# Two row tiles' sources moved into the first span of a graph-attention layer, and its settling scaled on ScalarE

## The chip, the cores and the metric

The kernel runs on one core of a Trainium2 chip. The metric is the device time of one execution in microseconds (us). Engines are named as in the profile: PE is TensorE's matmuls and PEld its weight loads, DVE is VectorE, ACT is ScalarE, POOL is GpSimd, SP is SyncE (here it issues most DMAs). A line number such as L1225 is a line of the kernel before.

## The reference, cut to what matters

Two layers run on 2708 nodes with 256 features. Each layer adds its result to its input and normalizes each row. Layer 0 is a diffusion with top-p attention; it is untouched by the change and only its last rows matter here. Layer 1 is a graph attention with four heads of 64:

```python
Wh = jnp.einsum('nd,hdo->nho', x, W)
s_i = jnp.einsum('nho,ho->nh', Wh, a_src)
s_j = jnp.einsum('nho,ho->nh', Wh, a_dst)
e = jax.nn.leaky_relu(s_i[:, None, :] + s_j[None, :, :], NEG_SLOPE)
mask = (adj.at[idx, idx].set(1.0) != 0)[:, :, None]
attention = jax.nn.softmax(jnp.where(mask, e, -jnp.inf), axis=1)
h_prime = jnp.einsum('ijh,jho->iho', attention, Wh)
x = _layernorm(x + h_prime.reshape(n, h * fo), axis=-1)
```

So every output row i is a sum over all source nodes j, divided by its softmax denominator per head, added to x and normalized.

## The kernel before, in words

The 2708 rows are cut into 22 row tiles: 16 of 128 rows and 6 of 110. `xe` holds x of all tiles in SBUF; layer 0 overwrites it tile by tile with its own result.

**End of layer 0.** The work of layer 0 is written as generators that a hand-made schedule advances slot by slot. `finish` (L919) is the last one of each tile: residual sums on GpSimd, two layernorms that go between VectorE (statistics L935, L936, output L944) and GpSimd (L940, the root L941), and then `sources` (L137). `sources` prepares a tile as a source of layer 1: TensorE transposes x (L142), ScalarE copies the transpose (L144), TensorE multiplies by the weights (L148), ScalarE writes the exponentials `sb` and `tj`, the scores `s_src` and the scaled values (L152 to L158), and SP stores the values in DRAM (L161). Its two PSUM tiles come from layer 0's pool `tr`.

**Layer 1.** Output rows are taken in three spans of 8, 8 and 6 row tiles (1024, 1024 and 660 columns). For each span the kernel goes over all 22 source tiles; the first span takes them in the order `first` (tiles 8 to 19, then 0 to 7, then 20 and 21). For each source tile:

- SP loads a block of the adjacency (L1164, three buffers `blk`), ScalarE makes a mask of it with Sign and Square (L1165, L1170), and where the block has the diagonal GpSimd sets it between the two (L1168, L1169);
- VectorE makes four products `pt`, one for each head (L1225), in two sets of buffers;
- TensorE accumulates the values (L1233, eight matmuls that use 64 columns of the array) and the denominators (L1240, eight that use 32 columns), in six PSUM banks `acc`.

`targets` (L167) prepares a span's rows: for each row tile four transposes (L174) into an `aux` bank and two exponentials on ScalarE (L179). For span 0 it runs in layer 0's last tile; for the next span it is called at the middle of a span (L1217). There are two `aux` banks in all.

At the end of a span ScalarE and VectorE copy the accumulators to SBUF as `val` and `den` (L1248 to L1250). `settle` (L1173) then finishes the span's row tiles. It is called at the third source tile of the next span (L1211), so that it lies beside that span's work, and at the very end for the last span (L1252). For each row tile: three transposes into an `aux` bank (L1180, L1181), the reciprocal of the denominators (L1183) and the scaling (L1187) on VectorE, the residual on GpSimd (L1192), layernorm (statistics L126 and L128 on VectorE, L130 and the root L132 on GpSimd, output L133 on VectorE), and a store by SP (L1195).

**What sets the order.** Each engine works through its own list in order. In layer 1 that list is made by a scheduler when the kernel is built, which can set an instruction ahead of the place where it is written: `targets` of span 1 is written at the middle of span 0, and in the list before it stands ahead of the span's first matmul, between the sources of the last tiles. A matmul that waits holds up all that stand behind it on TensorE.

A second, general version of layer 0 is run afterwards if a flag asks for it (L1261); with these inputs it is not run.

Of the kernel before, what the change touches and what calls it, by code (L numbers as in the profile page):

```python
# [16 lines left out]
P = 128  # L17
# [28 lines left out]
def kernel(  # L46
# [87 lines left out]
            dst, src, mv[:m, 0:1], rs[:m], op0=ALU.subtract, op1=ALU.mult  # L134
        )

    def sources(t, pool, ps):  # L137

        m = rows[t]
        tp = ps.tile([P, 4, P], F32, name="tr")  # L140
        for c in range(DC):
            nc.tensor.transpose(tp[:, c, :m], xe[:m, t, c * P : (c + 1) * P], ident[:m, :m])  # L142
        xT = pool.tile([P, DC, P], F32, name="xT")
        nc.scalar.copy(xT[:, :, :m], tp[:, 0:DC, :m])  # L144
        yield
        wp = ps.tile([P, 4, P], F32, name="tr").rearrange("p a b -> p (a b)")
        for c in range(DC):
            nc.tensor.matmul(  # L148
                wp[:m, : D + 2 * H], xT[:, c, :m], wx[:, c, :],
                start=(c == 0), stop=(c == DC - 1),  # L150
            )
        nc.scalar.activation(sb[:m, t, :], wp[:m, D : D + H], AF.Exp)  # L152
        nc.scalar.activation(tj[:m, t, :], wp[:m, D : D + H], AF.Exp, scale=NEG_SLOPE - 1.0)
        nc.scalar.copy(s_src[:m, t, :], wp[:m, D + H : D + 2 * H])
        vt = pool.tile([P, D], F32, name="cs")
        for h in range(H):
            cols = slice(h * FO, (h + 1) * FO)
            nc.scalar.activation(  # L158
                vt[:m, cols], wp[:m, cols], AF.Copy, scale=sb[:m, t, h : h + 1]
            )  # L160
        nc.sync.dma_start(vd[t][:m], vt[:m])  # L161
# [322 lines left out]
    def fast_layer0(ep, adjp):  # L484
# [434 lines left out]
        def finish(t, ac, ca, cb):  # L919

            m = rows[t]
            xt = xe[:m, t, 0:D]
            xw = rowp.tile([P, D], F32, name="xw")[:m]
            nc.scalar.activation(xw, ac[:m, :D], AF.Copy, scale=rinv[:m, t : t + 1])  # L924
            yield
            while t not in held:
                yield
            hh = heldp.tile([P, D], F32, name="hh", bufs=4)[:m]
            nc.gpsimd.tensor_add(ca[:m], ca[:m], cb[:m])
            nc.gpsimd.tensor_add(ca[:m], ca[:m], held.pop(t)[:m])  # L930
            nc.gpsimd.tensor_add(hh, ca[:m], xw)
            yield
            for last in range(2):
                st, mv = small.tile([P, 6], F32, name="ln_st")[:m], small.tile([P, 2], F32, name="ln_mv")[:m]
                nc.vector.bn_stats(st, hh)  # L935
                nc.vector.bn_aggr(mv, st)  # L936
                yield
                yield
                ve, rs = new("ln_ve", m), new("ln_rs", m)
                nc.gpsimd.tensor_scalar(ve, mv[:, 1:2], LN_EPS, None, op0=ALU.add)  # L940
                nc.gpsimd.tensor_tensor(rs, ve, minus_half[:m], op=ALU.pow)  # L941
                yield
                yield
                nc.vector.tensor_scalar(  # L944
                    xt if last else hh, hh, mv[:, 0:1], rs, op0=ALU.subtract, op1=ALU.mult
                )
                yield
                yield
                if not last:
                    nc.gpsimd.tensor_mul(hh, hh, g_sb[:m])  # L950
                    nc.gpsimd.tensor_add(hh, hh, b_sb[:m])
                    nc.gpsimd.tensor_add(hh, hh, xt)
                    yield
                    yield
            yield from sources(t, rowp, ps_tr)


# [30 lines left out]
                ),  # L988
            )

        ahead = []

        def step(s, cur, spend):
            for t in range(NT):
# [132 lines left out]
            bad, pt[0:1, 0:1], -1.0, float(2 * NT * P), op0=ALU.mult, op1=ALU.add  # L1127
        )
        l0.close()
        return ahead  # L1130

# [1 line left out]

    def layer1(ep, adjp, r):
        l1 = ExitStack()

        pp, rp, pj, keep = (
# [31 lines left out]
        def settle(g, val, den):  # L1173

            for t in spans[g]:
                m = rows[t]
                cols = slice(off[t] - off[spans[g][0]], off[t + 1] - off[spans[g][0]])
                u = ps_u.tile([P, H, P], F32, name="aux")
                for q in range(2):
                    nc.tensor.transpose(u[:m, q, :], val[:, q, cols], ident)  # L1180
                nc.tensor.transpose(u[:m, 2, :], den[:, cols], ident)  # L1181
                rden = small.tile([P, H], F32, name="rden")
                nc.vector.reciprocal(  # L1183
                    rden[:m], u[:m, 2, :].rearrange("p (h o) -> p h o", h=H)[:, :, 0]
                )
                res = pp.tile([P, H, FO], F32, name="res")
                nc.vector.tensor_tensor(  # L1187
                    res[:m], u[:m, 0:2, :].rearrange("p q (h o) -> p (q h) o", h=2),
                    rden[:m].unsqueeze(2).to_broadcast([m, H, FO]), op=ALU.mult,
                )  # L1190
                flat = res[:m].rearrange("p h o -> p (h o)")
                nc.gpsimd.tensor_add(flat, flat, xe[:m, t, 0:D])  # L1192
                o = pp.tile([P, D], F32, name="o")
                layernorm(o[:m], flat, m)
                nc.sync.dma_start(out[off[t] : off[t + 1], :], o[:m])  # L1195
# [5 lines left out]
        for g, span in enumerate(spans):  # L1201
            gw = off[span[-1] + 1] - off[span[0]]
            cuts = [(c, min(CHUNK, gw - c)) for c in range(0, gw, CHUNK)]
            acc = [
                [ps_v.tile([P, CHUNK], F32, name=f"acc{k}_{c}") for c in range(len(cuts))]
                for k in range(3)
            ]
            for n, j in enumerate(range(NT) if g else first):
                k = rows[j]
                if n == 2 and due:  # L1210
                    settle(*due)  # L1211
                if n == NT // 2 and g + 1 < len(spans):
                    if g % 2:
                        r_next = room(ep)
                    else:
                        r_next = [rp.tile([P, 2, GW], F32, name=f"r{q}") for q in range(2)]
                    list(targets(g + 1, r_next, aux))  # L1217
                if g == 0:
                    nc.sync.dma_start(v[j][:k].rearrange("p h o -> p (h o)"), vd[j][:k])
                mask = neighbours(g, j)  # L1220
                at = dict(start=(n == 0), stop=(n == NT - 1), skip_group_check=True)
                pts = []
                for h in range(H):
                    pt = pj.tile([P, GW], F32, name=f"pt{h}")
                    nc.vector.scalar_tensor_tensor(  # L1225
                        pt[:k, :gw], r[h // 2][:k, h % 2, :gw], tj[:k, j, h : h + 1], mask,
                        op0=ALU.max, op1=ALU.mult,
                    )
                    pts.append(pt)
                    if h % 2 == 1:  # L1230
                        for c, (c0, w) in enumerate(cuts):
                            for q in range(2):
                                nc.tensor.matmul(  # L1233
                                    acc[h // 2][c][q * FO : (q + 1) * FO, :w],
                                    v[j][:k, h - 1 + q, :],
                                    pts[h - 1 + q][:k, c0 : c0 + w], **at,
                                )
                for c, (c0, w) in enumerate(cuts):
                    for h in range(H):
                        nc.tensor.matmul(  # L1240
                            acc[2][c][h * 32 : (h + 1) * 32, :w],
                            sb[:k, j, h : h + 1].to_broadcast([k, 32]), pts[h][:k, c0 : c0 + w], **at,
                        )
            r = r_next
            val = pp.tile([P, 2, GW], F32, name="val")
            den = pp.tile([P, GW], F32, name="den")
            for c, (c0, w) in enumerate(cuts):
                nc.scalar.copy(val[:, 0, c0 : c0 + w], acc[0][c][:, :w])  # L1248
                nc.vector.tensor_copy(val[:, 1, c0 : c0 + w], acc[1][c][:, :w])
                nc.scalar.copy(den[:, c0 : c0 + w], acc[2][c][:, :w])  # L1250
            due = (g, val, den)
        settle(*due)  # L1252
        l1.close()
# [1 line left out]
    with ExitStack() as both:  # L1255

        adjp = both.enter_context(tc.tile_pool(name="adjp", bufs=3))
        ep = both.enter_context(tc.tile_pool(name="ep", bufs=3))
        layer1(ep, adjp, fast_layer0(ep, adjp))
    flag = nc.values_load(bad[0:1, 0:1])  # L1260
    with tc.If(flag > 0):  # L1261
        general_layer0()
        with ExitStack() as again:
            adjp = again.enter_context(tc.tile_pool(name="adjp", bufs=3))
            ep = again.enter_context(tc.tile_pool(name="ep", bufs=3))
            layer1(ep, adjp, None)


# [43 lines left out]
```

## Time and profile before

| what | before |
|---|---|
| median of three runs | 1677.54 us (1677.26 to 1679.2) |
| the profiled execution | 1677.58 us, of which the profile's span is 1675.8 us |
| layer 1's first matmul | 1298.14 us from the span's start |
| last matmul of the last span | ends near 1653.8 us |
| last output row tile written by VectorE | ends at 1668.76 us |

Times inside the profile are counted from the span's start. In the chain of waits each line gives start, length, engine, the tile written and the line. In lists by engine, "x16" counts profile records; a matmul of float32 has two records, a transpose one. The share of time an engine is busy is an average over stages with different limits, so the stages of layer 1 (1298 to 1676 us) are looked at one by one.

### The profile page before, as it was taken

How to read it: one execution, taken by the hardware profiler on the slowest of the kernel's cores; microseconds unless marked ns; L12 is line 12 of the kernel's file. 1: busy time of each engine (PE TensorE's matmuls, PEld its weight loads, DVE VectorE, ACT ScalarE, POOL GpSimd, SP SyncE). 2: the span in 40 equal slices, each digit the busy share in tenths (PEclk: the TensorE clock that was granted, in tenths of full speed). 3: DMA queues.
4: the chain of work that ended last, by engine and by line, in shares of the span. 5: the costliest groups of instructions: out<-in, count | busy, mean ns of one | idle time of the engine just before them, and what ended most of it. 6: DMA issues, size and time to landing. Idle time of an engine off the chain costs nothing.

```text
span 1675.8 us, 23985 instructions
## 1 busy us (share of the span) xinstructions
PE 1610.0 (96%) x8218; PEld 1058.0 (63%) x8218; DVE 1217.0 (73%) x3660; ACT 766.8 (46%) x1324; POOL 423.4 (25%) x893
## 2 busy tenths in 40 slices
PE   7999999999999999999999999999997999999895
PEld 4677777777777776777787878777785222322332
DVE  2954554565455019888999999998994899888886
ACT  1333333333333255656576666667555334243231
POOL 0310111111011023223244444444434020420313
PEclk9999999999999999999999999999999999999998
DMA  6211011111110142212322322323222332232231
GB/s 166 73 47 46 26 43 40 40 31 40 40 43 25 43 104 67 63 49 73 79 72 79 87 68 82 89 58 77 72 65 88 98 99 86 88 93 77 76 86 39
DMA packets 153873, 113.89 MB, mean 68 GB/s; under 512 B 39898, under 2 KB 144094, under 8 KB 153742
## 3 DMA queue, kind: packets, MB, share of 16 engines
q1 hardware_dynamic: 149278, 105.18, 23.4%
q0 software_dynamic: 2112, 5.55, 1.0%
q10 hardware_dynamic: 2352, 1.54, 0.3%
q8 instruction: 67, 1.10, 0.3%
q14 instruction: 64, 0.52, 0.1%
HBM read 101.16 MB, written 11.09 MB: 67 GB/s over the span
## 4 chain that ended last, share of the span: by engine, by line
PE 78%; DVE 9%; ACT 5%; POOL 4%; issue 3%; DMA 0%; ACTq 0%; POOLq 0%; DVEq 0%; SPq 0%
PE att L217 23%; PE walk L845 19%; PE acc L1233 12%; PE acc L1240 6%; PE lg L620 5%; PE tr L202 4%; ACT e L624 3%; PE tr L910 2%; PE tr L890 2%; PE lg L1056 1%; PE tr L591 1%; DVE cand L725 1%; ACT eT L208 1%; DVE scr L791 1%; POOL res L1192 1%
## 5 line engine op out<-in xcount | busy, mean ns | idle before, releaser
L645 ACT ACTIVATE junk<-e,minus,rth 128x2708 bf16<-128x2708 f32 (+1 forms) x88 | 232.8, 2646 | 35.7 <-POOL rth L677 34.6
L845 PE MATMUL walk<-xe,blk 128*128 128x257 f32 (+3 forms) x968 | 240.5, 382 | 0.0
L217 PE MATMUL att<-ba,eT 128*128 128x256 f32 (+3 forms) x968 | 234.1, 383 | 5.0 <-ACT eT L208 5.0
L217 PE MATMUL att<-xe,eT 128*128 128x256 f32 (+3 forms) x968 | 233.3, 381 | 4.3 <-ACT eT L208 4.3
L208 ACT COPY eT<-tr 128x512 f32<-128x512 f32 (+5 forms) x264 | 138.2, 537 | 206.3 <-PE tr L202 206.1
L1233 PE MATMUL acc<-pt,v 128*64 128x512 f32 (+3 forms) x1056 | 226.0, 550 | 4.7 <-DVE pt L1225 3.8
L845 PE MATMUL walk<-yw,blk 128*128 128x256 f32 (+3 forms) x968 | 228.1, 381 | 1.7 <-ACT xw L924 1.7
L725 DVE MAX8 cand<-e 128x8 f32<-128x170 f32 (+1 forms) x352 | 89.2, 322 | 178.8 <-ACT e L624 178.8
L845 PEld LDWEIGHTS walk<-xe,blk 128*128 128x128 f32 (+3 forms) x968 | 174.6, 186 | 54.2 <-issue 29.3
L845 PEld LDWEIGHTS walk<-yw,blk 128*128 128x128 f32 (+3 forms) x968 | 176.7, 186 | 41.5 <-issue 11.5
L1225 DVE SCALAR_TENSOR_TENSOR pt<-e,tj,blk 128x1024 f32<-128x1024 f32 (+3 forms) x176 | 185.8, 1115 | 19.8 <-issue 8.0
L217 PEld LDWEIGHTS att<-ba,eT 128*128 128x128 f32 (+3 forms) x968 | 171.4, 186 | 32.7 <-ACT eT L208 10.0
L217 PEld LDWEIGHTS att<-xe,eT 128*128 128x128 f32 (+3 forms) x968 | 170.9, 186 | 30.9 <-ACT eT L208 7.2
L624 ACT ACTIVATE e<-lg 128x1024 f32<-128x1024 f32 (+1 forms) x132 | 121.1, 921 | 132.3 <-PE lg L620 132.3
L1233 PEld LDWEIGHTS acc<-pt,v 128*64 128x64 f32 (+1 forms) x1056 | 72.1, 137 | 153.5 <-issue 112.3
L202 PE MATMUL tr<-ident,e 128*128 128x128 f32 (+3 forms) x968 | 140.8, 270 | 4.6 <-ACT xT L606 3.8
L202 PEld LDWEIGHTS tr<-ident,e 128*128 128x128 f32 (+3 forms) x968 | 115.1, 139 | 32.3 <-ACT xT L606 6.1
L1165 ACT ACTIVATE blk<-blk 128x1024 f32<-128x1024 f32 (+3 forms) x66 | 63.2, 958 | 155.3 <-DMA blk<-in_adjT_dram 136.3
L1240 PE MATMUL acc<-pt,sb 128*32 128x512 f32 (+3 forms) x1056 | 124.5, 549 | 0.0
L1225 DVE SCALAR_TENSOR_TENSOR pt<-r,tj,blk 128x1024 f32<-128x1024 f32 (+1 forms) x88 | 109.8, 1306 | 10.8 <-issue 7.0
L631 POOL TENSOR_TENSOR fact<-zp 128x1 f32<-128x1 f32 (+1 forms) x44 | 24.8, 563 | 359.0 <-ACT e L624 349.1
L725 DVE MAX8 cand<-scr 128x8 f32<-128x97 f32 (+1 forms) x616 | 101.9, 243 | 0.0
(203 smaller groups left out, 1999.6 us busy)
## 6 DMA issues: line engine op xcount, KB each, us to landing
blk<-in_adjT_dram SPq DMA_DIRECT2D x32, 704.0 KB
blk<-in_adjT_dram SPq DMA_DIRECT2D x32, 512.0 KB
blk<-in_adjT_dram SPq DMA_DIRECT2D x48, 330.0 KB
blk<-in_adjT_dram SPq DMA_DIRECT2D x32, 320.0 KB
blk<-in_adjT_dram SPq DMA_DIRECT2D x12, 605.0 KB
blk<-in_adjT_dram SPq DMA_DIRECT2D x12, 440.0 KB
blk<-in_adjT_dram SPq DMA_DIRECT2D x18, 283.6 KB
c<-cs POOLq DMA_DIRECT2D x32, 128.0 KB, 2.1
```

The costliest lines, as they stand in the source:

```text
L202: nc.tensor.transpose(tr[: rows[t], q, :m], e[:m, off[t] : off[t + 1]], ident[:m, :m])
L208: copy(eT[:k, : len(grp), :m], tr[:k, : len(grp), :m])
L217: nc.tensor.matmul(acc, eT[: rows[t], q, :m], value(t), start=(t == 0), stop=(t == NT - 1),)
L620: nc.tensor.matmul(lg[:m, h, :w], qT[part, cols], kT[s][part, c0 : c0 + w], start=True, stop=True,)
L624: nc.scalar.activation(halves[:m, :, c0 : c0 + w], lg[:m, :, :w], AF.Exp, accum_out=zp[:m, n : n + 1],)
L645: nc.scalar.activation(junk[:m], e[:m], func, scale=rth, bias=minus1[:m], accum_out=acc)
L725: nc.vector.max(cand[:, n, :], src[:m, n * size : min(N, (n + 1) * size)])
L845: nc.tensor.matmul(ac[:m, :w], blk[: rows[j], j - j0, :m], cur[: rows[j], j, 0:w], start=(j == 0), stop=(j == NT - 1),)
L1165: nc.scalar.activation(bar, bar, AF.Sign)
L1225: nc.vector.scalar_tensor_tensor(pt[:k, :gw], r[h // 2][:k, h % 2, :gw], tj[:k, j, h : h + 1], mask, op0=ALU.max, op1=ALU.mult,)
L1233: nc.tensor.matmul(acc[h // 2][c][q * FO : (q + 1) * FO, :w], v[j][:k, h - 1 + q, :], pts[h - 1 + q][:k, c0 : c0 + w], **at,)
L1240: nc.tensor.matmul(acc[2][c][h * 32 : (h + 1) * 32, :w], sb[:k, j, h : h + 1].to_broadcast([k, 32]), pts[h][:k, c0 : c0 + w], **at,)
```

## The change

The change has these parts.

- For the fast layer 0, `sources` of the last two row tiles (20 and 21) is not called at the end of `finish`. It is called in layer 1, at the third source tile of span 0, with layer 1's pools: the PSUM tiles are `aux` banks.
- `settle` scales on ScalarE: four activations of 64 columns for each row tile, with the reciprocal as scale, in the place of one VectorE instruction.
- In the last span's `settle` each of the six row tiles has a PSUM bank of its own (the `acc` banks, which are free by then), and the residual is added on VectorE. In the other spans GpSimd keeps it.
- Of the two copies of the denominators at the end of a span, the second moves from ScalarE to VectorE.

```diff
@@ finish
+            if t in late:
+                return
             yield from sources(t, rowp, ps_tr)
@@ fast_layer0
-        ahead = []
+        ahead, late = [], (NT - 2, NT - 1)
@@ settle
-                u = ps_u.tile([P, H, P], F32, name="aux")
+                if g < len(spans) - 1:
+                    u = aux()
+                else:
+                    n = t - spans[g][0]
+                    u = ps_v.tile([P, CHUNK], F32, name=f"acc{n // 2 % 3}_{n % 2}")
+                    u = u.rearrange("p (h m) -> p h m", h=H)
...
-                res = pp.tile([P, H, FO], F32, name="res")
-                nc.vector.tensor_tensor(
-                    res[:m], u[:m, 0:2, :].rearrange("p q (h o) -> p (q h) o", h=2),
-                    rden[:m].unsqueeze(2).to_broadcast([m, H, FO]), op=ALU.mult,
-                )
-                flat = res[:m].rearrange("p h o -> p (h o)")
-                nc.gpsimd.tensor_add(flat, flat, xe[:m, t, 0:D])
+                flat = pp.tile([P, D], F32, name="res")[:m]
+                for h in range(H):
+                    nc.scalar.activation(
+                        flat[:, h * FO : (h + 1) * FO],
+                        u[:m, h // 2, (h % 2) * FO : (h % 2 + 1) * FO],
+                        AF.Copy, scale=rden[:m, h : h + 1],
+                    )
+                adder = nc.vector if g == len(spans) - 1 else nc.gpsimd
+                adder.tensor_add(flat, flat, xe[:m, t, 0:D])
@@ layer1, over the source tiles
                 if n == 2 and due:
                     settle(*due)
+                if n == 2 and g == 0:
+                    for t in late:
+                        for _ in sources(t, pp, ps_u, "aux"):
+                            pass
@@ layer1, end of a span
-                nc.scalar.copy(den[:, c0 : c0 + w], acc[2][c][:, :w])
+                copy = nc.vector.tensor_copy if c else nc.scalar.copy
+                copy(den[:, c0 : c0 + w], acc[2][c][:, :w])
```

More of the change, by code (lines that the diff above doesn't have):

```diff
@@ L135, in layernorm, with sources @@
         )
-    def sources(t, pool, ps):
+    def sources(t, pool, ps, name="tr"):
         m = rows[t]
-        tp = ps.tile([P, 4, P], F32, name="tr")
+        tp = ps.tile([P, 4, P], F32, name=name)
         for c in range(DC):
@@ L145, in sources @@
         yield
-        wp = ps.tile([P, 4, P], F32, name="tr").rearrange("p a b -> p (a b)")
+        wp = ps.tile([P, 4, P], F32, name=name).rearrange("p a b -> p (a b)")
         for c in range(DC):
@@ L1129, in fast_layer0, with layer1 @@
         l0.close()
-        return ahead
-    def layer1(ep, adjp, r):
+        return ahead, late
+    def layer1(ep, adjp, r, late):
         l1 = ExitStack()
@@ L1258 @@
         ep = both.enter_context(tc.tile_pool(name="ep", bufs=3))
-        layer1(ep, adjp, fast_layer0(ep, adjp))
+        layer1(ep, adjp, *fast_layer0(ep, adjp))
     flag = nc.values_load(bad[0:1, 0:1])
@@ L1265 @@
             ep = again.enter_context(tc.tile_pool(name="ep", bufs=3))
-            layer1(ep, adjp, None)
+            layer1(ep, adjp, None, ())
 _ARGS = [
```

## The prediction

> **What bounds the kernel now.** I read the profile in this order: busy shares, busy time by stage, the chain of work that ended last in the three places the edits touch, and the order of instructions on each engine there.
>
> ```profile
> PE 1610.0 (96%) x8218; PEld 1058.0 (63%) x8218; DVE 1217.0 (73%) x3660; ACT 766.8 (46%) x1324; POOL 423.4 (25%) x893
> ```
>
> TensorE is the average bound, but the edits lie where it is not. By stage (columns: length, then busy PE, PEld, DVE, ACT, POOL, clock, DMA share, GB/s):
>
> ```profile
> 1298.10:1428.60 130.50, 130.46 (x768) 35.60 (x768) 116.30 (x96) 52.89 (x54) 15.00 (x16) 1.00 0.33 95
> 1428.60:1472.90 44.30, 42.92 (x204) 13.33 (x200) 35.62 (x60) 12.14 (x19) 20.17 (x28) 1.00 0.28 85
> 1472.90:1562.60 89.70, 89.70 (x556) 25.77 (x552) 80.55 (x70) 36.20 (x43) 9.42 (x12) 1.00 0.30 85
> 1562.60:1603.10 40.50, 35.73 (x222) 13.55 (x218) 31.34 (x64) 9.79 (x13) 15.14 (x24) 0.96 0.27 77
> ```
>
> Rows 1 and 3 are plain stretches of layer 1: a row tile takes TensorE 5.44 us, back to back. Rows 2 and 4 are where the previous span is settled. There five row tiles take 44.3 us (5.44 each would be 27.2) and, up to 1599.47, 36.9 us (3.62 each: 18.1), although TensorE has only 24 settling transposes to add, some 3 us. So each settling costs about 14 us. The chain says why (start, us, what):
>
> ```profile
> 1564.30 1.93 POOL res L1192 x2
> 1566.23 0.02 issue
> 1566.26 0.43 DVE ln_st L126
> ...
> 1568.63 0.41 DVE o L133
> 1569.05 0.34 DVE res L1187
> 1569.39 0.07 issue
> 1569.46 1.94 POOL res L1192 x2
> ...
> 1591.33 0.97 PE acc L1240 x2
> ```
>
> Scale on VectorE, residual on GpSimd, statistics, root on GpSimd, output, next scale: a serial round of 5.16 us for two row tiles (5.54 in row 2), in which VectorE passes one `pt` product (L1225). The last line is a second loss: a denominator matmul alone among numerators. At the handover from layer 0 and at the end:
>
> ```profile
> 1294.42 0.42 DVE xe L944
> 1294.84 0.04 issue
> 1294.88 0.41 PE tr L142 x2
> ...
> 1298.14 1.90 PE acc L1233 x7
> ```
>
> ```profile
> 1660.71 0.71 POOL res L1192
> ...
> 1662.29 0.41 DVE o L133
> ```
>
> Layer 1's first matmul waits for the last tile's x, and in the tail two tiles go round every 4.55 us (`o` at 1657.74, 1662.29, 1666.85).
>
> **What the Trainium skill says.** *TensorEngine Tiling (Array Packing)*, Key Properties: column tiles run in parallel, and changing the tiling mode drains TensorE. The trace agrees: eight 64-column matmuls take 3.59 us (0.90 a pair), four 32-column ones 0.93, a lone one 0.97. *SBUF — State Buffer*, Who interferes with whom: a VectorE instruction with two SBUF inputs and a GpSimd one that reads SBUF block each other. Agrees: `ln_ve` takes 0.22 us, but 1.16 beside a `pt` (at 1450.32). No page prices the new ScalarE scaling better than L158, the same form: four in 0.80 us.
>
> **First span.** Two kinds of work move. Sources of tiles 20 and 21: on TensorE 2 transposes (0.25 us with their gap) and 2 matmuls (0.9 to 1.1) each; on ScalarE 8 instructions (1.4 us); on SP a store and a load, now behind mask loads five and six, with over a dozen row tiles until those two are used. And what moved without being named: the 32 transposes and 16 exponentials of `targets` for span 1. Today they run while TensorE waits for x of tiles 20 and 21 (3.89 us idle before 1288.40 alone); in the new order they stand at the span's twelfth tile.
> - *Start.* In the new order only tile 20's transposes stand before the first matmul: x is there at 1288.3, the second `pt` at 1289.4, so matmuls start near 1289.45, 8.7 us earlier. But VectorE's order is unchanged: `pt` three and four end at 1292.3 and 1293.6 (a bn_stats waiting for GpSimd is in front), the next four at 1296.0 to 1299.6. The new order also sets a lone denominator matmul inside the first two tiles (0.97 each). First tile done 1297.3 (after the fourth `pt`: 1.8 + 1.86), second 1303.85 (+1.85+0.97+1.88+1.86), then 1.3 for tiles 20 and 21, third with tile 21's matmuls inside (1.0, and a broken pair 0.9) near 1312.6. Before: 1314.45. So −1.85 us.
> - *Targets.* 32 × 0.11 = 3.5 us; a broken pair 0.9; TensorE waits about 0.3 for the exponentials, which stand behind a mask's Square that waits for GpSimd. +4.7 us. The cover (waiting at the handover) is gone, so all of it counts. Bounds 3.5 to 7: the seventh and eighth groups stand behind a mask load.
>
> Net +2.85; bounds −3 to +6.
>
> **Settling into span 1.** VectorE loses L1187, 8 × 0.34 = 2.7 us, and gains one denominator copy (0.65), hidden in the 0.6 us a tile that it idles. ScalarE gains 8 × 0.80 = 6.4 us; it is idle 32 of these 44 us. Each scaling waits for its reciprocal, and masks (Sign, Square) queue behind it; they have some 5 us before VectorE needs them. GpSimd keeps the residual. The new VectorE order has eight `pt` in four rounds, where there were about four. My round: `pt` 1.6 (slowed by the residual add) and 1.2, two bn_stats 0.7, two outputs 0.7 to 1.0, small ones 0.35, two waits for the root 0.55 + 0.75: 6.2 us for two `pt`, against 5.54 for one. Walked through, the fourth tile's four `pt` end at 1430.0, 1431.75, 1433.85, 1436.65, the fifth's at 1440.1, 1442.9, 1446.3, 1449.1, the sixth's at 1452.5, 1455.15, 1456.35, 1457.9 (before: 1461.0). TensorE's order is nearly regular from the fifth tile on (before, lone 64- and 32-column matmuls in two tiles), so that it follows VectorE: sixth tile done 1461.6 (+1.8+1.86), seventh 1467.0 against 1472.92. −5.9. But 16 of the 24 transposes of span 2's targets, which were in this stretch, now stand with the other 8 at mid-span: 24 × 0.11 = 2.6, broken pair 0.9, wait 0.6, less the 0.9 that stands there today: +3.2. Net −2.7; bounds −5 to +3.
>
> **Settling into span 2.** The same with `pt` of 0.83 us: two `pt` with the add 2.1, statistics 0.7, small 0.35, waits and outputs 0.65+0.35+0.55+0.35: 5.05 us a round, with two `pt` instead of one. Last `pt` of the fourth tile 1567.1, fifth 1577.0, sixth 1585.75, seventh 1590.2 (before 1593.6); TensorE, with a lone denominator left in two tiles, is done at 1593.05 against 1599.47; 0.4 back for the denominator copy, since VectorE has only 0.26 us a tile to spare. −6.0; bounds −8.5 to +1. After that TensorE is back to back to 1653.8, so all of it reaches the end.
>
> **Tail.** Transposes go in one run (a bank each; today TensorE waits 0.72, 2.52 and 1.48 us for aux buffers). First scaling from 1654.85, 0.80 each, ahead of VectorE. VectorE adds: no row shows that add from SBUF; at least the 0.34 of L1187, at most GpSimd's 0.71; I take 0.35, as the same engine does it. First output 1657.93, later by 0.2; round add 0.35, stats 0.35, add 0.35, aggregate 0.10, root 0.99, output 0.35, aggregate 0.10, root 0.99, output 0.35 = 3.95 against 4.55. Last output ends 1667.7 against 1668.76: −1.05; bounds −2 to +0.8.
>
> **Sum.** +2.85 −2.7 −6.0 −1.05 = −6.9. The profiled execution took 1677.58 us with a span of 1675.8 (1.8 around it), and the median shown is 1677.54: 1670.7 us.
>
> **Rivals.**
> 1. *The start pays in full.* If lone matmuls cost nothing and the third tile keeps the 8.7 us less 2.6 for tiles 20 and 21, the start gives −6.1 instead of −1.85: 1666.4. For: TensorE is idle at the handover. Against: VectorE's times there don't move. 0.13.
> 2. *The settling gains only a third (no change).* The new order sets a `pt` before most statistics and outputs; if GpSimd's adds come late by half a `pt`, 8 us of the 11.9 gross go: 1678. For: `ln_ve` at 1.16 us. Against: the rounds already pay for that. 0.20.
> 3. *Slower.* Place: VectorE in the two settlings. If every row tile there waits once more for GpSimd's `ln_ve` and `ln_rs` behind a `pt` (0.77 us, as the last two outputs do today, at 1452.17 and 1454.61), 16 × 0.77 = 12.3 comes back, while the targets at mid-span keep costing: 1683. It decides from 0.64 us a row tile. Against: in the new order the add is issued earlier than the statistics. 0.13.
> 4. *Late sources don't free the start* (the change doesn't do that part): tile 20's transposes still stand first. If the first matmul waits until 1294.4, the last x, the third tile ends near 1314: 1672, inside my own case.
>
> **How the numbers follow.** My case 0.54, rivals 0.13, 0.20, 0.13. A measurement here tells about 0.2% (3.4 us) from no change. Faster: my case and rival 1, 0.67; same: rival 2, 0.20; slower: 0.13. Range 1664 to 1679: it reaches to rivals 1 and 2 and leaves out the slower one and the outer bounds. My case alone: 1665 to 1674.
>
> **What would show it.** First matmul of layer 1 near 1289.5, third tile done near 1312.6; the twelfth tile of span 0 about 10 us long; the seven tiles' end near 7 us and 6 us nearer to their span's start in spans 1 and 2; two `pt` a round; outputs in the tail every 3.95 us. Wrong, if `ln_st` waits for GpSimd's residual by more than 0.6 us a tile, if `blk` masks become what `pt` waits for (ScalarE's scalings in front of them), or if the twelfth tile takes over 13 us.

## The result: no change in time, and the profile after

The changed kernel takes 1680.26 us (median of 6, 1677.70 to 1683.43), the kernel before on the same chip 1677.56 us. The ratio is 1.0016, 95% interval 1.0002 to 1.0030: within the 0.2% that I had called no change, 9.6 us above the forecast of 1670.7 and just outside its range. A later series with 21 runs gave 1681.44 us, ratio 1.0015 (1.0009 to 1.0022). The changed kernel also scatters more: 6.6 us between its fastest and slowest of those 21, 3.3 us for 49 runs of the kernel before.

The profiled execution of the changed kernel took 1678.29 us with a span of 1676.4, against 1675.8 before. So two things have to be explained: why this execution is 0.6 us longer where −6.9 was forecast, and why the median lies another 2 to 3 us higher. For the second the evidence is less direct: this execution and the second one profiled (1677.22 us) are among the fastest of the changed kernel, and none of 1681 us or more was profiled.

Busy time of all engines in the profile after, and then the four stages of layer 1 between the same source tiles as the four rows shown of before (columns: length, then busy PE, PEld, DVE, ACT, POOL, clock, DMA share, GB/s):

```profile
PE 1611.0 (96%) x8218; PEld 1057.3 (63%) x8218; DVE 1213.5 (72%) x3647; ACT 784.7 (47%) x1409; POOL 422.2 (25%) x887
```

```profile
1290.20:1434.00 143.80, 143.57 (x812) 42.01 (x811) 123.24 (x105) 58.51 (x83) 15.83 (x20) 0.99 0.32 94
1434.00:1473.30 39.30, 36.86 (x190) 10.57 (x186) 32.31 (x53) 16.98 (x42) 21.15 (x26) 1.00 0.31 94
1473.30:1566.40 93.10, 92.81 (x573) 27.36 (x569) 82.46 (x72) 37.94 (x50) 12.66 (x14) 1.00 0.29 82
1566.40:1603.50 37.10, 34.51 (x222) 13.14 (x220) 29.08 (x58) 17.25 (x46) 15.39 (x24) 1.00 0.31 86
```

The settlings (rows 2 and 4) did become shorter: 39.3 us for 44.3, 37.1 for 40.5. The plain stretches became longer: row 1 takes 143.8 us for 130.5 (it begins 7.9 us earlier), with TensorE at work nearly all of the time; row 3 takes 93.1 for 89.7. A source tile is finished when TensorE ends its last denominator matmul (L1257 after, L1240 before). From those ends:

| piece | before, us | after, us | change | forecast |
|---|---|---|---|---|
| layer 0: its last statistics but one (L935) at | 1284.50 | 1285.77 | +1.27 | 0 |
| from there to span 0's third tile done | 30.02 | 28.31 | −1.71 | −1.85 |
| span 0: twelfth tile | 5.44 | 11.21 | +5.77 | +4.7 |
| span 1: third to seventh tile | 44.28 | 39.28 | −5.00 | −5.9 |
| span 1: twelfth tile | 6.34 | 9.75 | +3.41 | +3.2 |
| span 2: third to sixth tile | 32.11 | 27.25 | −4.86 | −6.4 with the next row |
| span 2: seventh tile | 4.74 | 5.05 | +0.31 | |
| span 2: eighth tile | 3.62 | 4.74 | +1.12 | +0.4 |
| last matmul to last output | 14.96 | 15.26 | +0.30 | −1.05 |
| sum | | | +0.6 | −6.9 |

All other source tiles take the same in both. The first row is no part of the change: other executions with late sources have it between −0.69 and +0.94. It goes with a stretch near 1263 us in which TensorE's granted clock is 0.50: in the eight profiles of this document where that lasts 6.83 us, L935 starts at 1285.32 to 1285.77, in the six where it lasts 3.41 us at 1283.81 to 1284.74. Every other sign but the last is as forecast, and nearly every piece fell short on the same side. What the pieces look like:

**Handover.** TensorE's instructions in order of time (start, length, what, idle time before it and what ended it):

```profile
1289.67 0.60 PE L142 MATMUL aux<-ident,xe 110*128 110x110 f32 x2 [4.45 <-DVE xe L944]
1290.20 3.61 PE L1250 MATMUL acc<-pt,v 128*64 128x512 f32 x8
```

and the stretch around them (columns as above):

```profile
1286.30:1292.90 6.60, 3.23 (x9) 1.79 (x10) 4.43 (x7) 0.10 (x1) 5.47 (x6) 0.50 0.55 164
```

Layer 1 starts 7.9 us earlier, and nearly all of that is lost again by the third tile, as forecast. The granted clock is 0.50 after the idle time, and four matmuls that take 1.8 us otherwise take 3.61. That costs nothing here: in another execution of this kernel the half clock lasts 3.41 us instead of 6.83, and the third tile is done 28.31 us after L935 in both, since VectorE's products set the pace.

**Settling into span 2.** One round on VectorE, with GpSimd's adds in it:

```profile
1574.00 2.62 DVE L1242 SCALAR_TENSOR_TENSOR pt<-e,tj,blk 128x660 f32<-128x660 f32 x2
1576.54 0.74 DVE L126 BATCH_NORM_STATS2 ln_st<-res 128x6 f32<-128x256 f32 x2
...
1578.36 0.41 DVE L133 TENSOR_SCALAR o<-res,ln_mv,ln_rs 128x256 f32<-128x256 f32 x1 [0.80 <-POOL ln_rs L132]
1579.23 0.41 DVE L133 TENSOR_SCALAR o<-res,ln_mv,ln_rs 128x256 f32<-128x256 f32 x1 [0.46 <-POOL ln_rs L132]
1579.56 2.19 DVE L1242 SCALAR_TENSOR_TENSOR pt<-e,tj,blk 128x660 f32<-128x660 f32 x2
```

```profile
1579.87 2.37 POOL L1205 TENSOR_TENSOR res<-res,xe 128x256 f32<-128x256 f32 x2 [0.68 <-ACT res L1198]
```

Two `pt` a round, as forecast, in 5.56 us (1574.00 to 1579.56) and then 5.43 us instead of 5.05. TensorE's lone denominator matmuls stand in three tiles behind it, the sixth, seventh and eighth:

```profile
1588.39 1.04 PE L1257 MATMUL acc<-pt,sb 128*32 128x512 f32 x2
...
1595.19 1.04 PE L1257 MATMUL acc<-pt,sb 128*32 128x512 f32 x2
...
1599.93 1.04 PE L1257 MATMUL acc<-pt,sb 128*32 128x512 f32 x2
```

**Tail.** VectorE:

```profile
1659.95 0.41 DVE L133 TENSOR_SCALAR o<-res,ln_mv,ln_rs 110x256 f32<-110x256 f32 x1 [1.00 <-POOL ln_rs L132]
1660.28 0.42 DVE L1205 TENSOR_TENSOR res<-res,xe 110x256 f32<-110x256 f32 x1
...
1661.44 0.43 DVE L1205 TENSOR_TENSOR res<-res,xe 110x256 f32<-110x256 f32 x1 [0.28 <-ACT res L1198]
...
1664.46 0.41 DVE L133 TENSOR_SCALAR o<-res,ln_mv,ln_rs 110x256 f32<-110x256 f32 x1 [1.00 <-POOL ln_rs L132]
```

and the ScalarE instructions between them:

```profile
1660.48 0.93 ACT L1198 ACTIVATE res<-acc,rden 110x64 f32<-110x64 f32 x4 [0.57 <-DVE o L133]
```

An output every two tiles comes at 4.51 us (1659.95 to 1664.46), not 3.95. The second scaling of a pair cannot start before the output `o` of the round before has read its `res` buffer: there are two such buffers.

### The profile page after: what moved, and what is told of

It reads as the page before. It is cut to its first block, busy times and chain, and to the rows that moved or that the text cites. A ratio compares the mean times of both kernels' runs of the same rounds, so it can differ in the third digit from the quotient of the medians.

```text
span 1676.4 us, 24051 instructions
## 1 busy us (share of the span) xinstructions
PE 1611.0 (96%) x8218; PEld 1057.3 (63%) x8218; DVE 1213.5 (72%) x3647; ACT 784.7 (47%) x1409; POOL 422.2 (25%) x887
## 5 line engine op out<-in xcount | busy, mean ns | idle before, releaser
L1250 PE MATMUL acc<-pt,v 128*64 128x512 f32 (+3 forms) x1056 | 231.4, 552 | 3.9 <-DVE pt L1242 3.7
L1257 PE MATMUL acc<-pt,sb 128*32 128x512 f32 (+3 forms) x1056 | 120.8, 548 | 0.0
```

Of the source, the lines that this page charges most:

```text
L1250: nc.tensor.matmul(acc[h // 2][c][q * FO : (q + 1) * FO, :w], v[j][:k, h - 1 + q, :], pts[h - 1 + q][:k, c0 : c0 + w], **at,)
L1257: nc.tensor.matmul(acc[2][c][h * 32 : (h + 1) * 32, :w], sb[:k, j, h : h + 1].to_broadcast([k, 32]), pts[h][:k, c0 : c0 + w], **at,)
```

## Experiments

### Which part pays, which part costs

Three kernels: the changed one again; the late sources alone on the kernel before; the change without the late sources.

```diff
-        ahead, late = [], (NT - 2, NT - 1)
+        ahead, late = [], ()      # the change without the late sources
```

The kernel again: 

> The changed kernel once more, unaltered. Theory (the loss and the gain are built into the order of work, and the scatter is the granted clock of TensorE, which fell to half in stretches of 3.4 or 6.8 us after TensorE had idled): the source tiles end as in the first profile of the changed kernel within 0.2 us, counted from the start of their span (twelfth tile of span 0 at 11.2 us, settling into span 2 27.3 us for the third to sixth tile), except where a stretch at half clock falls; median 1678 to 1683. Rival (the scatter is a wait on a transfer that comes late in some executions): other gaps before the products, and masks named as what ends them.

The late sources alone: 

> The kernel before with the late sources alone, settling as before. Theory (the late sources push the transposes and exponentials of the next span's targets into the span's twelfth tile, and this is what eats the change): span 0 longer by 5 us, its twelfth tile about 11 us; time 1682 to 1685. Rival (the late sources free the start and the loss sits in the settling): 1677 or less.

The rest alone: 

> The changed kernel without the late sources, so with the settling and the tail of the change alone. Theory: span 0 as in the kernel before, with the 32 target transposes at the handover; span 1 1.6 and span 2 3.4 us shorter than before, tail 0.3 longer: about 1673. Rival (the loss sits in the settling): 1678 or more.

| kernel | median, us | range | ratio to before (95%) |
|---|---|---|---|
| changed, again | 1681.44 (21 runs) | 1676.78 to 1683.36 | 1.0015 (1.0009 to 1.0022) |
| late sources alone | 1683.53 (5) | 1681.62 to 1688.37 | 1.0039 (1.0026 to 1.0053) |
| change without late sources | 1675.91 (21) | 1672.20 to 1677.61 | 0.9985 (0.9979 to 0.9992) |

The late sources are the loss. Alone they cost 5.8 us, and without them the changed kernel is 5.5 us faster: the settlings' gain was real. In the profile of the late sources alone the third tile is again done 28.31 us after L935, the twelfth takes 11.10 us, and all pieces from there to the end are within 0.05 us of the kernel before. In the settling alone the first span is that of before and the settlings are 39.28 and 27.25 us, the same as in the changed kernel. Its median is 3 us above the 1673 that I expected, and its mid-span shows why: the eighth to eleventh tile take 22.26 us and the twelfth 11.74 where the changed kernel took 21.75 and 9.75. TensorE has the same instructions in the same order there, but in the twelfth tile it waits 2.28 us for exponentials (L179) instead of 0.29; the 0.5 us before it is a broken pair in the ninth tile. The "again" profile shows such a wait at the other place of targets: the twelfth tile of span 0 takes 12.33 us for 11.21, not within the 0.2 us that I had expected. First TensorE there in the first profile, then TensorE and ScalarE in "again":

```profile
1359.83 1.20 PE L174 MATMUL aux<-ident,s_src 128*128 128x128 f32 x8 [0.23 <-ACT r L179]
```

```profile
1358.98 1.20 PE L174 MATMUL aux<-ident,s_src 128*128 128x128 f32 x8 [1.34 <-ACT r L179]
```

```profile
1353.32 1.06 ACT L1169 ACTIVATE blk<-blk 128x1024 f32<-128x1024 f32 x1 [0.20 <-DMA blk<-in_adjT_dram]
1357.32 1.06 ACT L1174 ACTIVATE blk<-blk 128x1024 f32<-128x1024 f32 x1 [2.94 <-POOL blk L1173]
1358.29 1.19 ACT L179 ACTIVATE r<-aux 128x256 f32<-128x256 f32 x4
```

The targets' exponentials (L179) need only the transposes, but they stand on ScalarE behind a mask's Square (L1174). That waits for GpSimd to set the diagonal (L1172, then L1173), and GpSimd waits for Sign and for the mask's transfer. GpSimd's second instruction in the first profile, with VectorE beside it, and in "again":

```profile
1357.68 0.45 POOL L1173 TENSOR_TENSOR blk<-blk,ident 128x128 f32<-128x128 f32 x1
1357.65 5.15 DVE L1242 SCALAR_TENSOR_TENSOR pt<-e,tj,blk 128x1024 f32<-128x1024 f32 x4 [0.36 <-issue]
```

```profile
1355.90 1.39 POOL L1173 TENSOR_TENSOR blk<-blk,ident 128x128 f32<-128x128 f32 x1
```

TensorE's idle time at this place was 0.23 us in the first profile, here 1.34. Counted from the tile's first transpose, the Square is 1.11 us later. GpSimd's two instructions make 1.03 of that: 1.37 and 1.39 us, for 1.28 and 0.45. Sign, which the transfer releases, starts only 0.09 us later. In the first profile L1173 starts at the end of a gap of 0.36 us between VectorE's products; in "again" a product is running. So the expectation that only the clock would differ fell, and here its rival, a late transfer, does too. In the settling alone the transfer has a part: of the 1.99 us by which the Square of the twelfth tile of span 1 is later than in the changed kernel, Sign is 0.96 late, and the rest is GpSimd's (2.20 us for 1.18, L1173 1.31 for 0.46).

### The targets at the handover again

```diff
+                if n == 0 and g == 0:
+                    r_next = [rp.tile([P, 2, GW], F32, name=f"r{q}") for q in range(2)]
+                    list(targets(1, r_next, aux))
```

(and no longer at the middle of span 0). 

> The changed kernel with the targets of span 1 asked for before the first source tile, so that their 32 transposes stand at the handover again and the late sources stay. Theory (the targets cost 5.8 us at the twelfth tile and are nearly free while TensorE waits for x at the handover): span 0 5 us shorter than in the changed kernel, 1672 to 1675. Rival (the exponentials or the broken pairs at the handover delay the first tiles as much): 1677 to 1681, the third source tile done at 1318 us or later.

Measured 1678.40 us (13 runs), ratio 1.0001 (0.9993 to 1.0009): 3 us better than the changed kernel, but the rival was nearer (its third tile was to be done at 1318 us or later; it was at 1317.25). The twelfth tile is back at 5.44 us, and the third is done 31.86 us after L935, 3.55 later than in the changed kernel and 1.84 later than before. At the handover both parcels of work do not fit: the late sources buy nothing once the targets are back. This profile also has a long wait at mid-span of span 1, first on TensorE and then on ScalarE:

```profile
1493.82 1.07 PE L1250 MATMUL acc<-pt,v 128*64 128x512 f32 x2
1497.17 1.51 PE L174 MATMUL aux<-ident,s_src 110*128 110x110 f32 x8 [2.29 <-ACT e L179]
1498.62 1.98 PE L1250 MATMUL acc<-pt,v 128*64 128x512 f32 x4
```

```profile
1495.58 1.06 ACT L1174 ACTIVATE blk<-blk 128x1024 f32<-128x1024 f32 x1 [2.41 <-POOL blk L1173]
```

After 2.29 us of idling the clock records show a stretch of 3.41 us at half speed from 1497.4: eight transposes 1.51 us for 1.0, the two matmuls after them 1.98 for 1.08. That tile took 13.22 us.

### The targets where no mask waits

```diff
-                if n == NT // 2 and g + 1 < len(spans):
+                if n == (6, 19)[g % 2] and g + 1 < len(spans):
```

> The changed kernel with the targets asked for where no mask has a diagonal to be mended: at the seventh source tile of span 0 and the twentieth of span 1. Theory (the exponentials of the targets stand on ScalarE behind a mask's Square, which waits for GpSimd, which waits for the mask's Sign and transfer; how late that transfer is differs between executions, so TensorE waits 0.2 to 2.3 us there and can then fall to half clock; this is the scatter): the seventh tile takes 10.9 us without a wait of TensorE, the twentieth 9.5; the runs lie within 3 us, around 1677.5. Rival (the scatter is the clock's own, at the handover): runs still from 1677 to 1683, median above 1680.

1676.97 us (13 runs), all between 1675.80 and 1678.25; ratio 0.9995 (0.9986 to 1.0003). The 6.6 us of scatter are now 2.45, and the median is 4.5 us below the changed kernel, although the targets cost nearly the same: eight tiles around the seventh take 48.87 us for 43.50, ten around the twentieth 58.22 for 54.38, so +5.4 and +3.8; in the first profile of the changed kernel it was +5.8 and +4.3. This profile has the same two stretches of half clock of 6.83 us at layer 0's end and at the handover as the first one of the changed kernel. So it is the place behind masks with a diagonal that makes the scatter and the 2 to 4 us between that profile and the median; the clock alone does not. That the wait for the Square is what the longer executions of the changed kernel have in common is not shown, since none was profiled; the 2.28 and 2.29 us in two of its variants speak for it, and so does a third one below.

### The targets of span 2 inside the settling, and more buffers

On the change without the late sources:

```diff
-                if n == NT // 2 and g + 1 < len(spans):
+                if n == (NT // 2, 4)[g % 2] and g + 1 < len(spans):
```

> Settling and tail of the change, sources of the last tiles where they were before, and the targets of span 2 asked for at the fifth source tile of span 1, inside the settling, where TensorE waits anyway. Theory: the 6.8 us that the targets cost at mid-span in the profile of the settling alone go, at most 3 come back inside the settling: 1667 to 1671. Rival (transposes and exponentials in the settling delay the scalings and so the whole round): 1674 or more, third to seventh tile of span 1 over 43 us.

and four buffers for `res`, with that and without it:

```diff
-                flat = pp.tile([P, D], F32, name="res")[:m]
+                flat = pp.tile([P, D], F32, name="res", bufs=4)[:m]
```

> As the kernel with the targets in the settling, and four buffers for `res` instead of two. Theory (the round in the settlings is a chain: a scaling waits for the output two row tiles back to free its `res` buffer, then the add, the statistics, the root and the output follow): third to sixth tile of span 2 2 us or more shorter than 27.25 us, tail 1 us shorter than 15.3, in all 2 to 5 us faster than with two buffers. Rival (VectorE's own work makes the round, as forecast): within 1 us of the kernel with two buffers.

> Settling and tail of the change, sources where they were before, four buffers for `res`; the targets of span 2 at mid-span. Theory (chain through the buffers): settling stretches of both spans 2 us or more shorter than 39.28 and 27.25 us; 1671 to 1674. Rival (VectorE's work): 39.3 and 27.3 us, about 1676.

| kernel | median, us (5 runs) | ratio to before (95%) | span 1, tiles 3 to 7 | span 2, tiles 3 to 6 | tail |
|---|---|---|---|---|---|
| targets in the settling | 1671.46 | 0.9957 (0.9943 to 0.9970) | 41.19 | 27.26 | 15.27 |
| and four `res` | 1666.78 | 0.9933 (0.9920 to 0.9947) | 38.25 | 28.11 | 12.78 |
| four `res`, targets at mid-span | 1670.95 | 0.9958 (0.9945 to 0.9972) | 38.24 | 28.09 | 12.94 |

Inside the settling the targets cost 1.9 us, and the twelfth tile is plain (5.44); the time is just above the 1667 to 1671 expected. The buffers shorten the tail by 2.5 us and the settling into span 1 by 2.9 (1.0 with the targets at mid-span), but span 2's settling becomes 0.8 us longer. So the two `res` buffers were the chain in the tail; in span 2 more of them did not help, and both expectations of 2 us there were wrong. The profiled execution of the last kernel in the table is its slowest, 1674.54 us, with the other four between 1670.66 and 1670.96. It has the mid-span wait, 2.33 us with a tile of 13.30 us, which is 3.55 more than the 9.75 of the changed kernel. In the tail the next limit shows in the chain of waits of the kernel with four:

```profile
1655.51 0.42 DVE o L133
1655.94 0.02 issue
1655.95 1.90 DMA out_dram<-o
...
1657.98 0.41 DVE o L133
```

The last output waits for an earlier output's transfer, which holds one of the two `o` buffers.

### More `o` buffers, and a mixture

```diff
-                o = pp.tile([P, D], F32, name="o")
+                o = pp.tile([P, D], F32, name="o", bufs=4)
```

> Targets in the settling, four buffers for `res` and four for `o`. Theory (with four `res` buffers alone the last output of the tail waited 1.19 us for the transfer of an earlier output to free its `o` buffer): tail 11.6 us after 12.8, time 1665.6, the settlings as with four `res` buffers alone. Rival (the root on GpSimd is as late as the buffer): tail over 12.4 us, time as with `res` alone, 1666.8.

and with two `res` buffers kept in the settling inside span 2: 

> As the kernel with four buffers of both kinds, but two `res` buffers for the settling of span 1's results, inside span 2. Theory (in span 2 more buffers change the order for the worse, 28.1 after 27.3 us): 27.3 us there, time 0.5 us below the kernel with four everywhere. Rival: no difference, within 0.3 us.

1668.16 us (1667.42 to 1669.57) and 1668.04 us (1666.84 to 1668.59): both more than with four `res` alone, whose runs lie between 1666.21 and 1666.90. The expectation was wrong: the tail is 13.80 and 13.77 us, and span 1's third to seventh tile take 39.30 and 39.28 us for 38.25. The transfer is no longer waited for, but with the buffers free the scheduler set VectorE's instructions in another order, in which each of the last outputs waits for its own root (0.69 to 1.00 us, outputs 1.5 to 2.2 us apart). Two `res` buffers inside span 2 do bring its tiles back to 27.22 us; in the median of the time that gain is not seen.

### What the scaling and the denominator copy are worth

Scaling back on VectorE in spans 1 and 2 (targets in the settling, two `res` buffers): 

> The kernel with the targets in the settling (third to seventh tile of span 1 41.2 us, third to sixth tile of span 2 27.3 us, 1671.5 us), but in spans 1 and 2 the scaling is done on VectorE as in the kernel before; tail, denominator copy and targets stay. Theory (the settlings gain because VectorE has no scaling to do): about 45 and 32 us, time 1679 to 1681. Rival (the gain comes from the copy of the denominators and the new place of the targets): 41 and 27 us, time 1671 to 1673.

1675.13 us (18 runs), ratio 0.9984 (0.9977 to 0.9991), so 3.7 us slower than with ScalarE's scaling and not the 7.5 to 9.5 expected (this series ran on another chip, where the kernel before takes 0.5 us less). Span 2's third to sixth tile 32.17 us against 27.26: there the scaling is the whole gain. The eighth tile is plain again (3.62). Span 1's third to seventh 42.28 against 41.19: there it is worth 1.1 us, and the rest of the gain over the 44.28 of before must lie in what else differs, the place of the targets and the copy; these were not tried apart with the scaling on VectorE.

Both denominator copies on ScalarE:

```diff
-                copy = nc.vector.tensor_copy if c else nc.scalar.copy
-                copy(den[:, c0 : c0 + w], acc[2][c][:, :w])
+                nc.scalar.copy(den[:, c0 : c0 + w], acc[2][c][:, :w])
```

> The kernel with the targets in the settling, both copies of the denominators on ScalarE as in the kernel before. Theory (in span 2 VectorE has little to spare, so the copy of 0.68 us and what it breaks of pairs is why the eighth tile still takes 4.74 us instead of 3.62): first to eighth tile of span 2 shorter by 0.7 to 1.1 us than 44.3 us. Rival (the lag comes from VectorE's products alone, or ScalarE's copy holds up the masks): 44.3 us or more.

1671.62 us against 1671.46, and span 2's first eight tiles take 44.2 us in both. With ScalarE's scaling the copy is free either way, so the theory was wrong; the eighth tile is still 4.74 us.

## Why the prediction was wrong, step by step

- **Start (−1.85; −1.71).** Right. VectorE's unchanged products and the lone matmuls take back all but 1.7 us of the earlier start (7.9 us, or 9.2 counted from L935). In four profiles with late sources and targets away from the handover the third tile is done 28.31 us after L935; what differs between them is when layer 0 ends. A thing that I had not looked at turned out to be harmless: the Trainium skill's page "TensorE: Matmul & The Clock Gate", Part 1, says that TensorE's clock falls to half after an idle window of about 3.4 us and stays there for as long at least, with a phase that varies between runs. The trace agrees: 0.50 for 3.41 or 6.83 us about the 4.45 us of idling.
- **Targets (+4.7; +5.77, more in other executions).** The named step failed in one number: "TensorE waits about 0.3 for the exponentials, which stand behind a mask's Square". It waited 0.23 there in the first profile and 1.34 in the second; the 32 transposes, at 1.0 to 1.1 us for eight instead of 0.9, and the broken pair make the rest. I read one wait as a constant, where the chain of transfer, Sign, GpSimd and Square has no slack and differs from run to run. The targets at mid-span of span 1 have the same wait: 0.29 us in both profiles of the changed kernel, 2.28 to 2.33 in three of its variants (0.6 forecast). When the targets were moved away from masks with a diagonal, 4.5 us went from the median, which takes it from above the kernel before to just below. For the median this is the largest error in the forecast; in the profiled execution the settling into span 2 (2.6 us) and the tail (1.35) are larger.
- **Settling into span 1 (−5.9; −5.0) and mid-span (+3.2; +3.4).** In this profile right within 1 us. A round took 6.28 us (outputs at 1446.55 and 1452.83) for 6.2. But my account, which gave VectorE's lost scaling as the cause, was too simple: the scaling itself is worth only 1.1 us where that was tried.
- **Settling into span 2 (−6.0; −3.4).** Two terms. The round was 5.4 to 5.6 us for 5.05: two `pt` beside GpSimd's adds took 2.5 us in the first of the two rounds (2.1 forecast), and the two waits for the root 1.26 for 1.20; the second round also waited 0.19 us for an add. And "a lone denominator left in two tiles" was wrong: there are three, and the eighth tile's is 1.12 us. Neither more `res` buffers nor the denominator copy took it away (4.74 us in both); with the scaling back on VectorE it is gone, so it comes with the order of work that ScalarE's scaling brings.
- **Tail (−1.05; +0.30).** The failed step is the round of 3.95 us, which let ScalarE scale ahead of VectorE for every pair. PSUM does allow that, with a bank for each tile, but `res` does not: its pool has two buffers. Before the change writer and last reader of `res` were both on VectorE, where the order alone kept them apart and no wait could be seen; I carried that over to two engines. With four buffers the tail is 12.78 us, more than the gain that I had forecast.
- **Rivals.** The outcome, no change, is rival 2's, and its time (1678) is the nearest, but not its mechanism: the settlings kept 8.4 of the 11.9 us gross. Rival 3's extra wait of 0.77 us a row tile did not come: the eight outputs wait 4.8 us for the root in all in span 1 and 5.6 in span 2, 5.3 each before. What put the median above the kernel before is none of the four: as far as the runs show, a wait in front of the moved targets. Rivals 1 and 4 did not come: the start paid its 1.7 us, no more and no less.

The version that stays is the change without the late sources, with span 2's targets inside the settling and four `res` buffers: 1666.78 us, 11.0 us or 0.7% below the kernel before in the same series.

## What to carry to other kernels

When work is moved onto another engine's queue, look at what stands ahead of it there and how far that is from being late: a wait of 0.2 us in one profile behind a transfer and two other engines was 1.3 us in the next execution, and more than 2 us at a like place in variants of the kernel. A wider scatter of the times was the sign of it. A gap that two parcels of work could use is filled once: here the targets had it, and the late sources only pushed them out to a place where every microsecond counts. And before an engine is counted as running ahead, count the buffers of what it writes.

## What the runs showed of the hardware

- TensorE's half-clock stretches up to the last matmul are 3.41 or 6.83 us long. In the 3.41 us before each that I looked at, TensorE was idle for part of the time only: 2.29 us before 1497.4 (shown above), 2.48 us before 1582.1 in the kernel before, 1.8 us before 1286.2 and 1.8 before 1262.3 in the changed one. So a stretch that is half idle can be enough, less than the Trainium skill's page "TensorE: Matmul & The Clock Gate", Part 1, says. The idle share alone does not decide: in the kernel before, 3.4 us with 1.8 us of idling near 647 us left the clock full. That idling is the cause is the page's statement; TensorE was not kept busy on purpose to try it.
- GpSimd's mending of the diagonal in spans 0 and 1 takes 0.45 us for an instruction that falls between VectorE's `pt` or starts together with one, and mostly 1.3 to 1.5 us where one is running; the residual add of two row tiles took 1.38 us (with four `res`) to 2.37 us.
- ScalarE's scaling from PSUM with a scale for each row costs 0.93 us for four instructions of 64 columns and 1.75 us for eight in the profile, so 0.82 for four more, near the 0.80 taken.
